# A three-layer CIN on one core: the weight tables built on the chip instead of gathered from HBM, and the first input tiles fetched by halves

## The chip, the core and the metric

The kernel runs on one core of one Trainium2 chip. The core has five engines that run side by side and wait for each other by semaphores: TensorE (PE, matrix products into PSUM), VectorE (DVE), ScalarE (ACT), GpSimd (POOL) and SyncE (SP), and 16 DMA engines that all queues share. The metric is device time of one launch in microseconds (us), lower is better. Everything is float32; each f32 matmul stands in the trace as two TensorE records.

## The reference, cut to what matters

```python
B, F, E, H = 1024, 39, 64, 64          # x is (1024, 39, 64); O = Hk = 64
def _cin_layer(Xk, X0, W, b):
    Wr = W.reshape(O, Hk, Fdim)
    return jnp.einsum('bhe,bfe,ohf->boe', Xk, X0, Wr) + b[None, :, None]
Xk = X0
for W, b in ((W0, b0), (W1, b1), (W2, b2)):
    Xk = _cin_layer(Xk, X0, W, b)
    outs.append(Xk.sum(axis=-1))
return jnp.concatenate(outs, axis=-1) @ fc_w.T + fc_b
```

Only linear sums of layers 2 and 3 are needed, so the kernel folds W1, W2 and fc_w into one table T. For each pair of fields (a, b) there is then one row of 128 weights, `T[a, b, 0:64]` beside `W0[a, b, 0:64]`. Because the product x_a·x_b is symmetric, the row for (a, b) is added to the row for (b, a). The hot loop multiplies pairs of rows of x (VectorE) and multiplies the products by these weights (TensorE).

## The kernel before

x is cut into 32 blocks of 2048 columns (32 samples of 64). A block is first copied to a DRAM table `xd` with one row for each field, and then GpSimd gathers four tiles of 128 rows, each a different list of fields (`rt`), so that six products of two tiles cover most pairs; a seventh product (`ut`·`vt`) covers the rest for two blocks at once. So two blocks have 13 steps: 12 of four full matmuls and one of eight half ones.

```python
def gather_rows(dst, n, k):
    table = xd[n // 2 % NTAB][: FT if k < 4 else 2 * FT]
    nc.gpsimd.indirect_dma_start(
        dst, None, table, bass.IndirectOffsetOnAxis(ap=lists[:, k : k + 1], axis=0))

def product(n, c):                       # VectorE, 128x2048
    p = prods.tile([128, BLK], F32, name="p", tag="p")
    ...nc.vector.tensor_tensor(p, rt[n % 2][:, i], rt[n % 2][:, k], ALU.mult)...

def multiply(n, c, p, quarters=range(BLK // MM)):     # TensorE, 512 columns each
    ...nc.tensor.matmul(po[n + h][m], wa[w, c, :], p[w, bass.ts(m, MM)], start=..., stop=...)
```

The weights go through DRAM. T is made by TensorE out of `w1s` and `v2`, joined with W0 in `part` and `rest`, stored as a DRAM table of 1600 rows, and gathered back twice for each of the seven chunks (the row of (a, b) into `wa`, that of (b, a) into `wb`); VectorE adds the two.

```python
for s, copy in enumerate((nc.vector.tensor_copy, nc.scalar.copy)):
    ...copy(part[:, :, at], pt[s]...); copy(rest[:, 0:NR, at], pr[s]...)
nc.sync.dma_start(tablev[:, 0:NA, :], part[0:FT])
nc.scalar.dma_start(tablev[:, NA : 2 * NA, :], part[H : H + FT])
nc.sync.dma_start(tablev[:, 2 * NA : FT, :], rest[0:FT])
...
def weights(c):
    for k, w in enumerate((wa, wb)):
        nc.gpsimd.indirect_dma_start(w[:, c], None, table[:],
            bass.IndirectOffsetOnAxis(ap=wlists[:, k, c : c + 1], axis=0))

weights(0); weights(1); weights(3)       # one GpSimd queue for weights and tiles
roll(1, (2,)); weights(2); roll(0, (3,)); weights(4); weights(5)
roll_half(0); weights(6); roll(1, (3,))
load(2); load(3)
...
nc.vector.tensor_tensor(wa[:, c], wa[:, c], wb[:, c], ALU.add)
```

The steps of the first two blocks are interleaved (three of block 0, three of block 1, then the rest), so that weights that come late are asked for late. `spin(n)` issues n matmuls of zeros into a bank that nobody reads. After that the loop is the same for all blocks: multiply step s, make the product of step s + 4, and at a block's end add its bias, multiply and reduce (`finish`, on ACT and DVE), then gather the tiles of block n + 2.

Of the kernel before, what the change touches and what calls it, by code (L numbers as in the profile page):

```python
# [57 lines left out]
FH = F * H  # L59
NG = 3  # L60
# [14 lines left out]
NA = 16  # L75
NR = F - 2 * NA
# [4 lines left out]
NONE = FT * FT - 1  # L81
# [14 lines left out]
def cin_kernel(ctx: ExitStack, tc: tile.TileContext, x, w0t, b0, w1, b1, w2, b2, fc_w, fc_b, out):  # L96
# [23 lines left out]
    def gather_rows(dst, n, k):  # L120
        table = xd[n // 2 % NTAB][: FT if k < 4 else 2 * FT]
        nc.gpsimd.indirect_dma_start(  # L122
            dst, None, table, bass.IndirectOffsetOnAxis(ap=lists[:, k : k + 1], axis=0)
        )

    def roll(n, tiles=range(4)):
        for i in tiles:
            gather_rows(rt[n % 2][:, i], n, n % 2 * 4 + i)
# [6 lines left out]
    wb = const.tile([128, NCHUNK, 2 * H], F32, name="wb")  # L135
    fc = const.tile([H, 3], F32, name="fc")
    v2 = const.tile([128, H], F32, name="v2")
    bias = const.tile([H, 2], F32, name="bias")
    b0s = const.tile([128, 1], F32, name="b0s")
# [5 lines left out]
    wlists = const.tile([128, 2, NCHUNK], I32, name="wlists")  # L145
# [4 lines left out]
    table = dram.tile([FT * FT, 2 * H], F32, name="table")  # L150
    tablev = table.rearrange("(b a) h -> b a h", a=FT)

    prep = tc.tile_pool(name="prep", bufs=1)
    with prep as prep:
        w2s = prep.tile([128, FH // 2], F32, name="w2s")
        w1s = prep.tile([128, FH // 2], F32, name="w1s")
        fc2 = prep.tile([128, 32], F32, name="fc2")
        ones = prep.tile([16, 128], F32, name="ones")
        zeros = prep.tile([128, MM], F32, name="zeros")
        w0s = prep.tile([128, NA * H], F32, name="w0s")  # L160
        w0r = prep.tile([H, NR * H], F32, name="w0r")
        part = prep.tile([128, NA, 2 * H], F32, name="part")
        rest = prep.tile([H, NR + 1, 2 * H], F32, name="rest")
        place = prep.tile([128, 1], I32, name="place")
        warm = prep.tile([1, 1], F32, name="warm")
# [3 lines left out]
        nc.vector.memset(warm, 0.0)  # L169
        nc.vector.memset(zeros, 0.0)  # L170
        nc.vector.memset(fc2, 0.0)  # L171
        nc.vector.memset(ones, 1.0)
        load(0, nc.gpsimd)
        nc.gpsimd.memset(w0s, 0.0)
        nc.gpsimd.memset(w0r, 0.0)
        load(1, nc.gpsimd)
        nc.gpsimd.memset(v2, 0.0)
        nc.gpsimd.memset(rest[:, NR], 0.0)

        def halves(dst, w):  # L180
            for s in range(2):
                nc.sync.dma_start(
                    dst[H * s : H * s + H], w[:, s * (FH // 2) : (s + 1) * (FH // 2)]
                )

        def load_ones(k, engine):
            for row in (F, FT + F):
                engine.dma_start(xd[k][row].rearrange("(p c) -> p c", c=128), ones)

        halves(w2s, w2)  # L190
        halves(w1s, w1)
        nc.scalar.dma_start(fc, fc_w.rearrange("o (l h) -> h (o l)", h=H))
        load_ones(0, nc.scalar)
        nc.scalar.copy(warm, warm)
        for k in range(2):
            nc.scalar.dma_start(w0s[H * k : H * k + F], w0t[:, NA * k : NA * (k + 1), :])
        nc.scalar.dma_start(w0r[0:F], w0t[:, 2 * NA : F, :])
        for s in range(2):
            nc.scalar.copy(fc2[H * s : H * s + H, 0:1], fc[:, 2:3])  # L199
            nc.scalar.copy(v2[H * s : H * s + H, F:FT], fc[:, 1:2])  # L200
        for k, t in enumerate((b1, b2)):
            nc.sync.dma_start(bias[:, k : k + 1], t.rearrange("(h o) -> h o", o=1))
        nc.sync.dma_start(b0s[H:128], b0.rearrange("(h o) -> h o", o=1))
        nc.sync.dma_start(fcb, fc_b.rearrange("(p o) -> p o", o=1))


        idle = bank("idle")

# [4 lines left out]
        spin(2)  # L213


        tmp = prep.tile([128, 16], F32, name="tmp")
        fields_of = prep.tile([128, 6], F32, name="fields_of")
        scaled = prep.tile([128, 6], F32, name="scaled")
# [16 lines left out]
        row, j, extra, t, half, q = new(), new(), new(), new(), new(), new()  # L235
        field = [fields_of[:, i : i + 1] for i in range(6)]
        nc.vector.tensor_copy(row, place)
        nc.vector.tensor_scalar(third, place, 171, None, ALU.mult)
        nc.vector.tensor_scalar(third, third, 9, None, ALU.logical_shift_right)
        nc.vector.tensor_copy(field[0], third)  # L240
        fused(j, field[0], -float(NG), row, ALU.mult, ALU.add)
        step(row, K, 1.0, extra)
        for i in (1, 2, 3):
            f = field[i]
            fused(f, j, float(STEP[i]), field[0], ALU.mult, ALU.add)
            step(f, F - BASE[i], -float(F), t)
            fused(f, f, float(BASE[i]), t, ALU.add, ALU.add)
            fused(t, row, float(EXTRA[i] - K), f, ALU.add, ALU.subtract)
            fused(f, t, extra, f, ALU.mult, ALU.add)
        nc.vector.tensor_scalar(t, field[0], -1.0, float(F), ALU.mult, ALU.add)  # L250
        fused(field[0], t, extra, field[0], ALU.mult, ALU.add)
        nc.vector.tensor_copy(lists[:, 0:4], fields_of[:, 0:4])
        nc.vector.tensor_scalar(lists[:, 4:8], fields_of[:, 0:4], float(FT), None, ALU.add)
        roll(0, (0, 1, 2))
        roll(1, (0, 1))
# [9 lines left out]

        nc.vector.tensor_scalar(half, half, float(FT), None, ALU.mult)
        nc.vector.tensor_scalar(lists[:, 8:10], fields_of[:, 4:6], half, None, ALU.add)

        blocks = prep.tile([H, F * 32], F32, name="blocks")
        w2v = w2s.rearrange("p (h f) -> p f h", f=F)
        pv = [bank("pv") for _ in range(2)]
        for k in range(2):
            for u in range(4):
                rows = slice(u % 2 * H, u % 2 * H + H)
                f0 = u // 2 * 19 + k * 10
                nc.tensor.matmul(  # L278
                    pv[k][32 * u : 32 * u + 32, 0:320],
                    fc2[rows],  # L280
                    w2v[rows, f0 : f0 + 10, :],
                    start=True,
                    stop=True,
                )
        spin(1)
        for k in range(2):
            for u in range(2):
                f0 = u * 19 + k * 10
                nc.vector.transpose(  # L289
                    blocks[:, 32 * f0 : 32 * (f0 + 10)], pv[k][H * u : H * u + H, 0:320]  # L290
                )
        column = blocks.rearrange("h (f j) -> h f j", j=32)[:, :, 0]
        nc.vector.tensor_copy(v2[0:H, 0:F], column)
        nc.scalar.copy(v2[H:128, 0:F], column)
        nc.scalar.copy(part[:, :, H : 2 * H], w0s.rearrange("b (a h) -> b a h", h=H))
        nc.scalar.copy(rest[:, 0:NR, H : 2 * H], w0r.rearrange("b (a h) -> b a h", h=H))


        nc.vector.tensor_scalar(scaled, fields_of, float(FT), None, ALU.mult)
        pair = prep.tile([128, 4], F32, name="pair")  # L300
        nc.vector.tensor_scalar(wlists[:, 0, 0:3], scaled[:, 1:4], field[0], None, ALU.add)
        nc.vector.tensor_scalar(wlists[:, 1, 0:3], fields_of[:, 1:4], scaled[:, 0:1], None, ALU.add)
        nc.vector.tensor_tensor(wlists[:, 0, 3:5], scaled[:, 2:4], fields_of[:, 1:3], ALU.add)
        nc.vector.tensor_tensor(wlists[:, 1, 3:5], scaled[:, 1:3], fields_of[:, 2:4], ALU.add)
        for m, (i, k) in enumerate(((1, 3), (3, 1), (4, 5), (5, 4))):
            nc.vector.tensor_tensor(pair[:, m : m + 1], scaled[:, k : k + 1], field[i], ALU.add)
        fused(wlists[:, 0, 5:6], extra, float(NONE), pair[:, 0:1], ALU.mult, ALU.max)
        fused(wlists[:, 1, 5:6], extra, float(NONE), pair[:, 1:2], ALU.mult, ALU.max)
        last = step(q, 62, float(NONE))
        nc.vector.tensor_tensor(wlists[:, 0, 6:7], pair[:, 2:3], last, ALU.max)  # L310
        nc.vector.tensor_scalar(t, q, float(F), float(NONE), ALU.is_lt, ALU.mult)
        nc.vector.tensor_tensor(pair[:, 3:4], pair[:, 3:4], t, ALU.max)
        nc.vector.tensor_tensor(wlists[:, 1, 6:7], pair[:, 3:4], last, ALU.max)


        w1v = w1s.rearrange("o (h f) -> o f h", f=F)
        pt = [bank("pt") for _ in range(2)]
        pr = [bank("pr") for _ in range(2)]
        for s in range(2):
            rows = slice(H * s, H * s + H)  # L320
            for k in range(2):
                nc.tensor.matmul(  # L322
                    pt[s][H * k : H * k + H],
                    v2[rows],
                    w1v[rows, NA * k : NA * (k + 1), :],
                    start=True,
                    stop=True,
                )
        for s in range(2):
            rows = slice(H * s, H * s + H)  # L330
            nc.tensor.matmul(  # L331
                pr[s][rows, 0 : 32 * NR], v2[rows], w1v[rows, 2 * NA : F, :], start=True, stop=True
            )
# [15 lines left out]
    def weights(c):  # L349
        for k, w in enumerate((wa, wb)):  # L350
            nc.gpsimd.indirect_dma_start(  # L351
                w[:, c], None, table[:], bass.IndirectOffsetOnAxis(ap=wlists[:, k, c : c + 1], axis=0)
            )

    weights(0)
    weights(1)
    weights(3)
    roll(1, (2,))
    weights(2)
    roll(0, (3,))  # L360
    weights(4)
    weights(5)
    roll_half(0)
# [191 lines left out]
```

## Time and profile before

| what | value |
|---|---|
| device time, median of 3 runs (range) | 768.59 us (768.55 to 769.1) |
| span of the profiled run, mean TensorE clock granted | 766.5 us, 0.991 |
| busy: PE, DVE, ACT, POOL | 745.1, 641.2, 160.4, 320.4 us |
| first matmul of the hot loop starts | 33.13 us |
| its last ones end | about 761.5 us |

Span and waits come from one profiled execution, the time from runs without a profile. The span is 2.1 us shorter than the device time. A group of instructions in the profile gives busy time, mean ns of one, idle time of its engine before them and what ended it. "PEld" is TensorE's weight load, which overlaps its matmuls. PEclk is the clock that the throttle granted, 1.00 is full speed.

### The profile page before, as it was taken

To read this page: it belongs to the slowest core of one execution; us is meant where nothing else is said; L and a number is where in the kernel's file an instruction comes from. 1 tells how busy PE (TensorE), PEld (TensorE's weight loads), DVE (VectorE), ACT (ScalarE), POOL (GpSimd) and SP (SyncE) were. 2 spreads that over 40 slices of the span, in tenths; PEclk is the share of its full clock that TensorE was granted. 3 is DMA by queue.
4 is the path that set the end of the run, shared out by engine and by line. 5 is a ranking of instruction groups with operands and counts; after the bars stand their busy time and mean duration, and the time that the engine had idled before them with its cause. 6 is when DMAs were issued, how large, how long until landed. Compare 5 with 4: busy or idle time off the path is not lost.

```text
span 766.5 us, 5146 instructions
## 1 busy us (share of the span) xinstructions
PE 745.1 (97%) x1856; PEld 322.3 (42%) x1856; DVE 641.2 (84%) x479; ACT 160.4 (21%) x207; POOL 320.4 (42%) x185
## 2 busy tenths in 40 slices
PE   6597999999999999999999999999999999999998
PEld 2243444444444444444444444444444444444443
DVE  5375988889888889888889988888988888998885
ACT  2002312122221212222121222112122221112212
POOL 4487273542436244253634325363442636334200
PEclk9899999999999999999999999999999999999999
DMA  8849958576865757676575777657577764737400
GB/s 260 268 151 384 402 183 342 168 273 231 327 240 203 283 170 276 244 316 241 189 287 183 276 254 292 256 178 284 185 297 252 267 260 147 284 150 317 165 0 0
DMA packets 62839, 181.79 MB, mean 237 GB/s; under 512 B 41364, under 2 KB 41499, under 8 KB 42254
## 3 DMA queue, kind: packets, MB, share of 16 engines
q0 software_dynamic: 23712, 169.34, 57.5%
q1 hardware_dynamic: 38494, 11.36, 6.4%
q10 hardware_dynamic: 608, 0.77, 0.3%
q8 instruction: 14, 0.23, 0.1%
q14 instruction: 11, 0.09, 0.0%
HBM read 180.58 MB, written 11.10 MB: 250 GB/s over the span
## 4 chain that ended last, share of the span: by engine, by line
PE 91%; DMA 3%; issue 2%; POOL 2%; DVE 1%; ACT 0%; DVEq 0%; POOLq 0%; SPq 0%
PE po L391 91%; DMA table<-rest 1%; POOL wa L351 1%; DMA u<-xd,lists 1%; POOL wb L351 1%; DMA wb<-table,wlists 0%; PE pt L322 0%; DVE blocks L289 0%; POOL r L122 0%; DVE fields_of L233 0%; DVE tmp L229 0%; DVE tmp L233 0%; PE pr L331 0%; DVE g L430 0%; DVE sums L432 0%
## 5 line engine op out<-in xcount | busy, mean ns | idle before, releaser
L391 PE MATMUL po<-p,wa 128*128 128x512 f32 (+1 forms) x1792 | 724.3, 597 | 11.9 <-DVE wa L471 11.9
L377 DVE TENSOR_TENSOR p<-r 128x2048 f32<-128x2048 f32 x192 | 434.5, 2291 | 88.1 <-PE po L391 82.2
L391 PEld LDWEIGHTS po<-p,wa 128*128 128x128 f32 (+1 forms) x1792 | 315.0, 190 | 420.4 <-issue 395.4
L122 POOL DMA_INDIRECT r<-xd,lists x128 | 249.3, 1948 | 366.0 <-DVE p L377 340.0
L410 ACT ACTIVATE x<-po,b0s 64x512 f32<-64x512 f32 x124 | 84.5, 684 | 356.4 <-PE po L391 349.8
L404 ACT COPY g<-u 39x1024 f32<-39x1024 f32 x64 | 66.6, 1043 | 216.2 <-DVE sums L421 181.2
L416 DVE SCALAR_TENSOR_TENSOR g<-po,fc,x 64x512 f32<-64x512 f32 x124 | 86.4, 734 | 0.0
L421 DVE TENSOR_REDUCE sums<-g 103x16 f32<-103x1024 f32 x62 | 75.6, 1220 | 2.2
L379 DVE TENSOR_TENSOR p<-u,v 128x2048 f32<-128x2048 f32 x16 | 36.5, 2284 | 9.1 <-DMA v<-xd,lists 9.1
L122 POOL DMA_INDIRECT u<-xd,lists x16 | 29.8, 1859 | 4.9 <-issue 4.6
L122 POOL DMA_INDIRECT v<-xd,lists x16 | 16.6, 1035 | 4.9 <-issue 4.9
L351 POOL DMA_INDIRECT wa<-table,wlists x7 | 11.0, 1573 | 14.6 <-DMA table<-rest 12.8
L211 PE MATMUL idle<-zeros 128*128 128x512 f32 x24 | 12.9, 686 | 1.5 <-DVE fc L171 1.5
L471 DVE TENSOR_TENSOR wa<-wa,wb 128x128 f32<-128x128 f32 x7 | 2.0, 291 | 11.6 <-DMA wb<-table,wlists 11.6
L351 POOL DMA_INDIRECT wb<-table,wlists x7 | 9.7, 1382 | 2.1 <-issue 2.1
L211 PEld LDWEIGHTS idle<-zeros 128*128 128x128 f32 x24 | 4.8, 212 | 8.2 <-issue 6.8
L430 DVE SCALAR_TENSOR_TENSOR g<-po,fc,x1q 64x512 f32<-64x512 f32 x4 | 3.0, 742 | 5.3 <-ACT x1q L429 5.3
L278 PE MATMUL pv<-w2s,fc 64*32 64x320 f32 x16 | 2.8, 764 | 4.5 <-ACT fc L199 4.5
L289 DVE STREAM_TRANSPOSE blocks<-pv 64x320 f32<-64x320 f32 x4 | 2.1, 514 | 3.7 <-issue 3.6
L429 ACT ACTIVATE x1q<-po,b0s 64x512 f32<-64x512 f32 x4 | 2.7, 684 | 10.2 <-PE po L391 10.2
L278 PEld LDWEIGHTS pv<-w2s,fc 64*32 64x32 f32 x16 | 1.0, 142 | 6.7 <-ACT fc L199 6.1
L432 DVE TENSOR_REDUCE sums<-g 103x8 f32<-103x512 f32 x4 | 2.7, 686 | 0.1
(74 smaller groups left out, 30.0 us busy)
## 6 DMA issues: line engine op xcount, KB each, us to landing
xd<-in_x SPq DMA_DIRECT2D x30, 312.0 KB
r<-xd,lists POOLq DMA_INDIRECT x128
w2s<-in_w SPq DMA_DIRECT2D x2, 312.0 KB
xd<-in_x POOLq DMA_DIRECT2D x2, 312.0 KB
w1s<-in_w SPq DMA_DIRECT2D x2, 312.0 KB
table<-part SPq DMA_DIRECT2D x1, 320.0 KB
table<-part ACTq DMA_DIRECT2D x1, 320.0 KB
w0s<-in_w0t ACTq DMA_DIRECT2D x2, 156.0 KB
```

Source lines behind the costliest of these rows:

```text
L122: nc.gpsimd.indirect_dma_start(dst, None, table, bass.IndirectOffsetOnAxis(ap=lists[:, k : k + 1], axis=0))
L211: nc.tensor.matmul(idle, zeros[:, 0:128], zeros, start=True, stop=True)
L278: nc.tensor.matmul(pv[k][32 * u : 32 * u + 32, 0:320], fc2[rows], w2v[rows, f0 : f0 + 10, :], start=True, stop=True,)
L351: nc.gpsimd.indirect_dma_start(w[:, c], None, table[:], bass.IndirectOffsetOnAxis(ap=wlists[:, k, c : c + 1], axis=0))
L377: nc.vector.tensor_tensor(p, rt[n % 2][:, i], rt[n % 2][:, k], ALU.mult)
L379: nc.vector.tensor_tensor(p, ut[n // 2 % 2], vt[n // 2 % 2], ALU.mult)
L391: nc.tensor.matmul(po[n + h][m], wa[w, c, :], p[w, bass.ts(m, MM)], start=c == opens[n + h], stop=c == closes[n + h],)
L404: nc.scalar.copy(gt[H : H + F], ut[n // 2 % 2][h : h + F, bass.ts(m, SUB)])
L410: nc.scalar.activation(x1[m // 2][:, bass.ts(m % 2, MM)], po[n][m][H:128], AF.Identity, bias=b0s[H:128])
L416: nc.vector.scalar_tensor_tensor(gt[0:H, at], po[n][m][0:H], fc[:, 0:1], x1[m // 2][:, at], ALU.add, ALU.mult)
L421: nc.vector.tensor_reduce(sums[:, b_at : b_at + SB], gt.rearrange("p (b e) -> p b e", e=E), AX.X, ALU.add)
L430: nc.vector.scalar_tensor_tensor(gt[0:H], po[n][m][0:H], fc[:, 0:1], t, ALU.add, ALU.mult)
```

## The change

It is for the opening. The DRAM table of weights, its 14 gathers, `wb`, and the lists of rows go away. Instead `both` holds the same table in SBUF, with h on the partitions (W0's 64 and T's 64) and the pair (a, b) along the row. A chunk's rows lie on diagonals of that table, so VectorE adds pieces of a diagonal to their mirror images into `pairs`, TensorE turns the 128x128 chunk, and ACT copies it to `wa`. W0's half of `both` comes from 39 TensorE transposes, T's half from 39 small matmuls. The first three tiles of block 0 are gathered by halves of 1024 columns and the first products are made by halves; block 0's steps now all come before block 1's. The first load moves from GpSimd's queue to ACT's, GpSimd's second load goes behind the first gathers, fc_w is loaded as one row and turned by TensorE, and 12 spins become three. W0 and T trade places in the 128 columns; `finish` is otherwise as it was.

```diff
+        for cols in halves:
+            roll(0, (0, 1, 2), cols)
+        load(1, nc.gpsimd)
+        roll(0, (3,))
 ...
+        roll(1, (0, 1))
+        roll_half(0)
+        roll(1, (2, 3))
+        load(2, nc.gpsimd)
+        load(3, nc.gpsimd)
 ...
-        nc.sync.dma_start(tablev[:, 0:NA, :], part[0:FT])
-        nc.scalar.dma_start(tablev[:, NA : 2 * NA, :], part[H : H + FT])
-        nc.sync.dma_start(tablev[:, 2 * NA : FT, :], rest[0:FT])
 ...
+        for a in range(F):
+            nc.tensor.transpose(at_field(a, 0)[:, 0:F], w0s[:, a * H : a * H + H], unit[0:F, 0:F])
+        for a in range(F):
+            nc.tensor.matmul(at_field(a, H), w1v[:, a, :], v2, start=True, stop=True)
+        for g in range(4):
+            at = slice(g * NG0 * FT, min((g + 1) * NG0, F) * FT)
+            copy = (nc.vector.tensor_copy, nc.scalar.copy)[g % 2]
+            copy(both[:, at], pt[g][:, 0 : at.stop - at.start])
+        spin(1)
 ...
-    weights(0)
-    weights(1)
-    weights(3)
-    roll(1, (2,))
 ...(and the rest of that list)
+    def weight_rows(c):
+        def put(at, by, n, a, b, sa, sb, twice=True):
 ...
+                nc.vector.tensor_tensor(
+                    out, diagonal(a, b, sa, sb), diagonal(b, a, sb, sa), ALU.add
+                )
 ...
+        for j in range(NG):
+            a, b = STEP[i] * j + BASE[i], STEP[k] * j + BASE[k]
+            cuts = sorted({0, F - a, F - b, F})
+            for lo, hi in zip(cuts, cuts[1:]):
+                put(NG * lo + j, NG, hi - lo, (a + lo) % F, (b + lo) % F, 1, 1)
+    def weight_turn(c):
 ...
+        nc.tensor.transpose(tr[:, at], pairs[:, c], unit)
+        nc.scalar.copy(wa[:, c], tr[:, at])
 ...
+    weight_rows(0)
+    weight_turn(0)
+    for k, (n, c) in enumerate(steps[:3]):
+        if k:
+            weight_rows(c)
+        p[n, c] = prods.tile([128, BLK], F32, name="p", tag="p")
+        product(n, c, halves[0], p[n, c])
+    for n, c in steps[:3]:
+        product(n, c, halves[1], p[n, c])
+    n, c = steps[3]
+    weight_rows(c)
+    p[n, c] = product(n, c)
+    for k, (n, c) in enumerate(steps[:3]):
+        multiply(n, c, p[n, c], (0,))
+        if k < 2:
+            weight_turn(steps[k + 1][1])
+        multiply(n, c, p[n, c], (1,))
```

In the loop the rows of chunks 5 to 7 are made just ahead of the product that needs them, and each turn stands after the first matmul of the step before.

## The prediction

> **What bounds the kernel now.** I read the page's first part, the costliest groups, ACT's timeline for the loop's period, then the chain of waits and the timeline of the first 70 us. First the page: engine totals, and the loop's matmuls and products.
>
> ```profile
> PE 745.1 (97%) x1856; PEld 322.3 (42%) x1856; DVE 641.2 (84%) x479; ACT 160.4 (21%) x207; POOL 320.4 (42%) x185
> ...
> L391 PE MATMUL po<-p,wa 128*128 128x512 f32 (+1 forms) x1792 | 724.3, 597 | 11.9 <-DVE wa L471 11.9
> L377 DVE TENSOR_TENSOR p<-r 128x2048 f32<-128x2048 f32 x192 | 434.5, 2291 | 88.1 <-PE po L391 82.2
> ```
>
> TensorE is the bound: ahead of the loop's matmuls it idled 11.9 us in all, for weights. VectorE waits for TensorE (82.2 us), not the reverse. ACT's timeline shows the period of two blocks, since ACT takes a block's banks as soon as TensorE closes them:
>
> ```profile
> 197.78 1.49 ACT L410 ACTIVATE x<-po,b0s 64x512 f32<-64x512 f32 x2 [13.16 <-PE po L391]
> ...
> 242.82 1.48 ACT L410 ACTIVATE x<-po,b0s 64x512 f32<-64x512 f32 x2 [13.16 <-PE po L391]
> ```
>
> That is 45.04 us for two blocks, 3.46 us a step, and it repeats unchanged to the end. Sixteen pairs are 16 x 45.03 = 720.5 us that the change doesn't touch. What is left is the opening. The chain of waits, in order of time:
>
> ```profile
> 17.07 0.35 ACT rest L338
> 17.49 10.15 DMA table<-rest
> 27.67 0.70 issue
> 28.36 0.95 POOL wa L351
> ...
> 29.62 0.42 POOL wb L351
> ...
> 53.30 7.05 DMA u<-xd,lists
> ...
> 66.10 0.30 DVE wa L471
> 66.44 695.02 PE po L391 x1728
> ```
>
> The weights are ready in SBUF at 17.4; 10.15 us go into storing the table, and five more into gathering it. Later the same queue of GpSimd, with weights and tiles in turn, brings u and then the last chunk so late (53.3 to 66.1) that TensorE waits once more. The timeline has the first product of the loop's matmuls, and the second stall:
>
> ```profile
> 19.17 2.29 DVE L377 TENSOR_TENSOR p<-r 128x2048 f32<-128x2048 f32 x1 [1.83 <-DMA r<-xd,lists]
> ...
> 33.13 12.08 PE L391 MATMUL po<-p,wa 128*128 128x512 f32 x24 [7.85 <-DVE wa L471]
> ...
> 66.44 34.12 PE L391 MATMUL po<-p,wa 128*128 128x512 f32 x82 [4.06 <-DVE wa L471]
> ```
>
> The first product starts at 19.17, so the inputs are there 14 us ahead of the weights. The stretch by stretch view shows the clock:
>
> ```profile
> 33.00:34.00 1.00, 0.87 (x1) 0.50 (x2) 1.00 (x1) 0.00 (x0) 0.70 (x2) 0.50 0.98 181
> ...
> 37.00:38.00 1.00, 1.00 (x4) 0.47 (x3) 0.00 (x0) 0.00 (x0) 0.69 (x2) 1.00 0.10 29
> ```
>
> At half clock (0.50, the third last column) for about 3.4 us after each of the two stalls, a loss of some 1.7 us each. So the balance is: start 33.1, plus 720.5, plus 4.06 idle and two half-clock stretches (together 7.8), ends at 761.4; the tail to 766.5 and 2.1 outside the span are 7.2 more: 768.6.
>
> **What the Trainium skill says.** (1) "TensorE: Matmul & The Clock Gate", Part 1: the clock starts at half rate, is released by some 3.4 us of activity, and falls back after idling. The trace agrees: 0.50 at 33 us, 1.00 from 37. Its Part 4 adds that transposes on TensorE may not count as activity; no instruction of the kernel before shows it. (2) The same page, "LDWEIGHTS": a load costs by its columns, P/1.2 ns, so 53 ns for 64. The trace has 131 ns for a 64-column f32 load, 190 ns for 128 and 78 ns for one, all at full clock: some 77 ns fixed and 0.9 ns a column. (3) "TensorEngine Tiling (Array Packing)", "Instruction Overhead": about 60 cycles a matmul however narrow. This bears on the 78 narrow products that are new. (4) "DMA: Bandwidth & Descriptors", "Anatomy of one DMA": about 2.0 us fixed beside the bytes. The table's way out and back pays this twice, and its 10.15 us for 800 KB are longer than that formula, since the queues were full (DMA share about 1.0 from 5 to 25 us).
>
> **Part by part.**
>
> *Removed.* The store (10.15 us), its issue gaps and the gathers up to the first addition: from 17.4 to 33.1, 15.7 us of the chain. Further on, twelve weight gathers that delay tiles on GpSimd's queue (about 1.25 to 2.2 us each), and with them the stall of 4.06 us at 62 to 66 and its cold stretch of 1.9.
>
> *When can weights exist now?* The loads ahead of the gathers are w2, w1 and one block of x, 1.6 MB against 1.93 MB before, with w0's 0.4 MB behind them. The profile moves 119 GB/s in the first 5 us and 267 in the next. I take w2 as landed at 7 (fc_w as one row no longer holds it up; before, the pv products waited until 9.77 on ACT). The pv products took 2.84 us at half clock; the same columns again: 10. Two VectorE transposes and copies, where four took 2.2 us: v2 at 11.2. Meanwhile TensorE turns W0: 39 transposes, then 39 matmuls x 2 records = 78. A pass has a 64-column load and 40 columns of moving data. Loads overlap the matmul before (in the loop a 190 ns load disappears in 433 ns records). Between full overlap (0.9 x 64 = 58 ns) and the whole 131 ns of a load I choose 90 ns: 39 x 90 = 3.5 us and 78 x 90 = 7.0 us. Whether a transpose is one record or two isn't shown in this trace; I take one. 10 + 3.5 + 7.0 = 20.5. A last short copy 0.3, six diagonal additions of about 0.1 us (four independent 128x1 additions take 0.42 us in this trace), 0.7 with a gap, then a first half product of 1.17 us (half of 2.29); the turn and its copy, some 0.6, lie beside that product. First matmul at about **22.5 us**, against 33.1.
>
> *Inputs.* Six half gathers of 0.5 MB, 1.25 us of GpSimd each, start when block 0 has landed, 7 to 9 us. At the 330 to 420 GB/s of this stretch all 3 MB are in by 18 to 19. So the halves are ahead of the weights and don't set the start.
>
> *Added after the start.* VectorE makes rows (0.6 to 1.0 us a chunk) among half products: rows and second half 2.0 us after the first, third 2.2 after that, while two matmuls take 1.7: about 0.7 us of TensorE gaps. Then the products come at 3.3 us a step, TensorE needs 3.46. Six turns on TensorE at 0.3 us (190 ns load and 128 columns): 1.8. One spin at full clock stands in the gap, so I count half of a cold stretch: 0.9. Tiles: tile 3, four more gathers and the rest are 8 MB from 19 us at 400 GB/s, u and v in by 34, needed near 38: no stall. Together 3.5 to 4.
>
> *Sum.* 22.5 + 720.5 + 4 + 7.2 = 754.2. I allow 0.8 for what a longer list of dependent starts usually adds: **755.0 us**, that is 13.6 less (1.8%).
>
> **Rivals.** (A) *The narrow passes are the new chain.* If a transpose is two records and a pass costs 131 ns or runs at half clock (few spins are left, and light passes may not release the clock), 117 to 156 passes take 15 to 20 us instead of 10.5, and the first matmul comes at 28 to 32: 760 to 765. For it: cold 128-column loads measure 340 ns here, and the pv products ran wholly at 0.50. Against: the store-and-gather detour it replaces was 15.7 us. (B) *Everything fits, and the inputs set the start.* Gathering by halves is only worth its trouble if tiles are late against weights; if passes take 60 ns, weights are done at 17, the first matmul comes at 18.5 to 19.5 and the time is 750 to 751. For it: the 39-column loads at 24.9 us follow each other within 80 ns. (C) *VectorE becomes the bound of the first block.* Some 50 strided additions on a path that also makes products; at 0.17 us each instead of 0.1 they add 3.5 us, of which a step's slack eats little: 757 to 758. (D) *The gain is returned later* because a tile comes late in blocks 1 to 3 or a PSUM bank is still held by the turned chunks: one stall of 3 to 5 us and a cold stretch, 759 to 761. The loop has no slack to recover anything, as TensorE sets every period.
>
> **Range and chances.** B pulls to 750, A to 763, C and D by a few us up. I give 748.5 to 762.0 for 8 in 10. The 2% line is near 753.4, a little below my centre, and B lies under it: 0.41 for faster by over 2%, 0.57 within 2%, 0.02 slower by over 2%; the last would need a start later than 45 us.
>
> **What would show it.** The period between ACT's block ends must stay 45.03 us; if not, the whole balance is wrong. The loop's first matmul should start at 19 to 26 us, waiting for VectorE's first half product, and no stall over 1.5 us should stand later. The 117 narrow passes should cost 60 to 130 ns each from start to start; over 10.5 us in all means A. The gathered halves must have landed before the first product is ready to go; if the product waits for DMA, B's view of inputs holds. Diagonal additions near 0.1 us refute C. I am wrong altogether if the new chain of preparation is longer than 30 us.

## The result, and the profile after

The changed kernel takes 756.75 us (median of 4 runs, 756.49 to 757.34) against 768.83 for the kernel before: a ratio of 0.984, 95% interval 0.983 to 0.986. That is 12.1 us less; 755.0 had been predicted, with a range of 748.5 to 762.0. The span of the profiled run is 754.8 us, the mean granted clock 0.990.

The page of the changed kernel, first its engine totals, then groups of instructions (busy us, mean ns of one, idle time ahead and what ended it):

```profile
PE 747.9 (99%) x1968; PEld 331.6 (44%) x1968; DVE 641.7 (85%) x506; ACT 160.9 (21%) x216; POOL 318.1 (42%) x184
...
L418 PE MATMUL po<-p,wa 128*128 128x512 f32 (+1 forms) x1792 | 723.2, 596 | 0.4 <-ACT wa L392 0.4
...
L339 PE MATMUL pt<-v,w1s 64*64 64x40 f32 x78 | 9.6, 312 | 0.0
...
L339 PEld LDWEIGHTS pt<-v,w1s 64*64 64x64 f32 x78 | 9.5, 213 | 0.1
...
L356 DVE TENSOR_TENSOR pairs<-both 128x6 f32<-128x6 f32 (+27 forms) x50 | 5.4, 175 | 0.4 <-ACT both L343 0.4
```

L418 is the loop's matmul (L391 before). Its idle time went from 11.9 us to 0.4: once the loop has begun, TensorE waits for no weights. The busy time is the same within 1.1 us. TensorE now has 112 more records, nearly all ahead of the loop. ACT's timeline shows that the loop itself is untouched:

```profile
71.56 1.48 ACT L437 ACTIVATE z<-po,fc0s 64x512 f32<-64x512 f32 x2 [9.29 <-PE po L418]
...
116.59 1.48 ACT L437 ACTIVATE z<-po,fc0s 64x512 f32<-64x512 f32 x2 [9.70 <-PE po L418]
```

Two blocks take 45.03 us, as before. The chain of waits (start, us, what), from the first spin on:

```profile
6.97 2.00 PE idle L210 x2
8.98 2.51 PE pv L305 x14
11.48 0.94 PE pt L333 x8
12.43 1.50 PE pt L337 x39
13.93 9.54 PE pt L339 x78
23.47 2.00 PE idle L210 x2
25.47 0.23 PE tr L391
...
25.72 0.27 ACT wa L392
...
26.04 2.07 PE po L418 x2
...
49.61 699.92 PE po L418 x1744
```

Compare this with the chain shown of before. No DMA stands in it from there to the end; the table's 10.15 us, its gathers and the 7.05 us of `u` are gone. In their place stands TensorE itself, from 7 to 26: the products for v2 (L305), zero products that clear the banks (L333), 39 transposes (L337), 78 narrow passes (L339), and twice a spin (L210). The loop begins at 26.04 instead of 33.13 (7.1 us), and from there to the end of its matmuls (749.5) it takes 723.5 us instead of 728.3 (4.8 us). These two make 11.9 of the 12.1 us. Of 723.5, 720.5 are the sixteen periods, so 3.0 us are lost after the start. The stretch by stretch view (after the span: busy share and count of PE, PEld, DVE, ACT, POOL, then the clock, DMA share, GB/s) has the larger part of that:

```profile
14.00:15.00 1.00, 1.00 (x10) 1.00 (x10) 0.00 (x0) 0.00 (x0) 0.92 (x1) 1.00 0.89 267
15.00:16.00 1.00, 1.00 (x11) 1.00 (x10) 0.00 (x0) 0.00 (x0) 0.77 (x1) 0.93 0.56 119
16.00:17.00 1.00, 1.00 (x10) 1.00 (x10) 0.00 (x0) 0.00 (x0) 0.69 (x2) 0.50 0.76 301
...
29.00:30.00 1.00, 1.00 (x3) 0.50 (x2) 1.00 (x2) 0.00 (x0) 1.00 (x1) 0.74 0.54 172
```

The clock falls to half near 15.9 us, in the middle of the narrow passes and with TensorE busy all the time, and comes back at about 29.5: 3.5 us of the loop at half speed lose some 1.8. Six turns at 0.11 to 0.21 us and three tiny products before 49.6 are another 1.1.

### The profile page after: what moved, and what is told of

Same layout as the page of the kernel before. It is cut to its first block, busy times and chain, and to the rows that moved or that the text cites. A ratio compares the mean times of both kernels' runs of the same rounds, so it can differ in the third digit from the quotient of the medians.

```text
span 754.8 us, 5372 instructions
## 1 busy us (share of the span) xinstructions
PE 747.9 (99%) x1968; PEld 331.6 (44%) x1968; DVE 641.7 (85%) x506; ACT 160.9 (21%) x216; POOL 318.1 (42%) x184
## 4 chain that ended last, share of the span: by engine, by line
PE 99%; DVE 1%; ACT 0%; issue 0%
PE po L418 96%; PE pt L339 1%; PE idle L210 1%; PE pv L305 0%; PE pt L337 0%; PE tr L391 0%; PE pt L333 0%; DVE g L457 0%; PE small L271 0%; DVE sums L459 0%; ACT zq L456 0%; PE small L267 0%; DVE zeros L184 0%; PE small L277 0%; DVE fcrow L265 0%
## 5 line engine op out<-in xcount | busy, mean ns | idle before, releaser
L418 PE MATMUL po<-p,wa 128*128 128x512 f32 (+1 forms) x1792 | 723.2, 596 | 0.4 <-ACT wa L392 0.4
L404 DVE TENSOR_TENSOR p<-r 128x2048 f32<-128x2048 f32 (+1 forms) x195 | 434.7, 2257 | 84.5 <-PE po L418 84.5
L418 PEld LDWEIGHTS po<-p,wa 128*128 128x128 f32 (+1 forms) x1792 | 314.5, 190 | 405.7 <-issue 384.2
L123 POOL DMA_INDIRECT r<-xd,lists x131 | 255.8, 1952 | 373.5 <-DVE p L404 326.6
L437 ACT ACTIVATE z<-po,fc0s 64x512 f32<-64x512 f32 x124 | 84.3, 683 | 356.5 <-PE po L418 349.7
L443 DVE SCALAR_TENSOR_TENSOR g<-po,b0s,z 64x512 f32<-64x512 f32 x124 | 86.3, 734 | 0.0
L123 POOL DMA_INDIRECT v<-xd,lists x16 | 25.8, 1612 | 4.9 <-issue 4.6
L339 PE MATMUL pt<-v,w1s 64*64 64x40 f32 x78 | 9.6, 312 | 0.0
L339 PEld LDWEIGHTS pt<-v,w1s 64*64 64x64 f32 x78 | 9.5, 213 | 0.1
L210 PE MATMUL idle<-zeros 128*128 128x512 f32 x6 | 6.2, 1140 | 1.7 <-DVE zeros L184 1.7
L356 DVE TENSOR_TENSOR pairs<-both 128x6 f32<-128x6 f32 (+27 forms) x50 | 5.4, 175 | 0.4 <-ACT both L343 0.4
L116 POOL DMA_DIRECT2D xd<-in_x x5 | 5.2, 1056 | 0.0
L456 ACT ACTIVATE zq<-po,fc0s 64x512 f32<-64x512 f32 x4 | 2.7, 683 | 10.2 <-PE po L418 10.2
```

What stands on the lines that cost most here:

```text
L116: engine.dma_start(xd[n // 2 % NTAB][first : first + F].rearrange("f (b e) -> f b e", e=E), xv[:, n * BB : (n + 1) * BB, :],)
L123: nc.gpsimd.indirect_dma_start(dst[:, cols], None, table, bass.IndirectOffsetOnAxis(ap=lists[:, k : k + 1], axis=0), element_offset=cols.s ...
L210: nc.tensor.matmul(idle, zeros[:, 0:128], zeros, start=True, stop=True)
L339: nc.tensor.matmul(at_field(a, H), w1v[:, a, :], v2, start=True, stop=True)
L356: nc.vector.tensor_tensor(out, diagonal(a, b, sa, sb), diagonal(b, a, sb, sa), ALU.add)
L404: nc.vector.tensor_tensor(p[:, cols], r[:, i, cols], r[:, k, cols], ALU.mult)
```

## The experiments

Three theories were open. **Chain:** the start is the sum of TensorE's small work, so each microsecond taken out of it comes off the time; within it either the stride of the weights in `w1s` (39 floats) or the half clock makes the passes dear. **Inputs:** the tiles set the start, so the chain is hidden. **Contention:** something beside the chain, the gathers above all, disturbs it. Kernels 1 to 4 ran on one chip, 5 to 8 on a second, 9 to 12 on a third, each beside the kernel before (767.93, 767.58, 768.31 us).

| kernel | time, us (range) | ratio to before (95%) | profiled run: first loop matmul | its device time less that start |
|---|---|---|---|---|
| changed kernel | 756.75 (756.49 to 757.34) | 0.984 (0.983 to 0.986) | 26.04 | 730.6 |
| 1 no spins | 758.74 (758.09 to 759.87) | 0.988 (0.986 to 0.990) | 28.16 | 731.7 |
| 2 contiguous weights | 758.15 (758.13 to 758.56) | 0.988 (0.986 to 0.990) | 28.26 | 729.9 |
| 3 without T | 754.69 (754.13 to 755.15) | 0.983 (0.981 to 0.985) | 22.66 | 731.5 |
| 4 whole gathers | 756.22 (755.41 to 756.92) | 0.985 (0.983 to 0.987) | 26.04 | 729.4 |
| 5 whole gathers and products | 758.78 (758.73 to 759.43) | 0.989 (0.987 to 0.992) | 27.69 | 731.7 |
| 6 gathers after the table | 761.84 (759.97 to 765.89) | 0.992 (0.989 to 0.995) | 30.99 | 734.9 |
| 7 five wide products | 761.26 (758.95 to 763.66) | 0.993 (0.989 to 0.996) | 29.66 | 730.8 |
| 8 the same, no spins | 759.08 (758.52 to 759.84) | 0.990 (0.987 to 0.992) | 28.21 | 731.6 |
| 9 first products early | 760.27 (759.06 to 761.35) | 0.990 (0.988 to 0.992) | 28.65 | 731.1 |
| 10 T ahead of W0 | 757.64 (756.49 to 758.37) | 0.987 (0.985 to 0.989) | 26.18 | 730.3 |
| 11 whole gathers, no spins | 757.08 (756.81 to 757.24) | 0.986 (0.984 to 0.987) | 25.30 | 731.7 |
| 12 changed kernel again | 759.17 (758.84 to 760.51) | 0.989 (0.987 to 0.990) | 30.07 | 730.4 |

The last column holds the whole study together: whatever is done to the opening, what comes after the start costs 729.4 to 731.7 us (number 6 has a late stall). The start decides the time, so the question is what decides the start. Within the 2.3 us of this column, it is mostly the length of the half-clock stretch that differs: 1.0 us after the start in kernel 4, 5.8 in kernel 11.

A caution for what follows: the changed kernel was measured on two occasions, and the times don't overlap (756.49 to 757.34, and 758.84 to 760.51 as number 12), though the kernel before took 768.83 and 768.31 beside them. Differences of about 2 us count only between kernels of one chip, and the changed kernel itself ran beside 9 to 11 alone.

**1. The spins ahead of the v2 products and after the table left out.**

```diff
-        spin(1)          # before the v2 products
...
-        spin(1)          # after the copies of the table
```

> The two spins after the first are left out. Chain theory (one queue of TensorE work ahead of the loop sets the start, and the time follows it one to one): the pv products start at 7.0 to 7.6 us instead of 8.98 if w2 has landed by then, and the last spin no longer stands between the diagonal additions and the first turn: first matmul of the loop at 23.8 to 24.4 instead of 26.04, time 754.5. If w2 lands only near 9, the last spin alone is gained: 756.4. Rival, clock: the spins are what lifts the clock; without them the loop's first stretch at half clock gets up to 2 us longer and eats the gain: 756 to 758.

Measured: 758.74 us. The v2 products start at 6.91, two microseconds earlier, so w2 was there and the spin had stood in front of it. But then the transposes wait 1.62 us for W0, which lands at 11.9, and start at 11.96 instead of 12.36: 0.4 of the 2 us is left. After that the narrow passes take 12.3 us instead of 9.5, since TensorE stops among them three times without a wait that the profile shows (0.40, 0.85 and 0.50 us, "issue"), with groups of only 3 to 5 passes between. The time lies above the range of the rival too. On this trace leaving the spins out gains nothing; what it is worth without the stops, kernel 11 shows.

**2. Weights of the narrow passes contiguous.** W1 is handed over laid out as (o, f, h); nothing else changes.

```diff
-        w1v = w1s.rearrange("o (h f) -> o f h", f=F)
+        w1v = w1s.rearrange("o (f h) -> o f h", h=H)
```

> w1 is laid out in memory with h innermost, so the weights of the 39 narrow products are 64 neighbouring floats instead of every 39th; nothing else changes. Stride theory: the 212 ns of these weight loads, the same before and after the clock fell at 15.9 us, come from the stride; contiguous they take 131 ns as in the kernel before, the 78 passes 5 us instead of 9.5, time 752 to 752.5. Rival, clock: at half clock contiguous 64-column loads take 222 to 227 ns as well (the zero and fc products), so only the passes before 15.9 get faster: the 78 passes take 8 to 9.5 us, time 755.5 to 756.7.

Measured: 758.15 us. Here is what the stride costs. The statistics of the weight loads (min/median/max ns of a record) in the changed kernel between 14.6 and 15.3 us, at full clock by the view above:

```profile
L339 PEld LDWEIGHTS pt<-v,w1s x8: 212/213/220, 14.4 to 15.3; 64*64 64x64 f32 x8
```

and the same of kernel 2, also at full clock:

```profile
L339 PEld LDWEIGHTS pt<-v,w1s x14: 135/135/135, 14.5 to 15.2; 64*64 64x64 f32 x14
```

A load of 64 columns takes 135 ns when its elements lie side by side and 212 when they are 39 floats apart, and the passes follow each other in 67 ns (21 in 1.41 us) instead of 122. At half clock the loads no longer differ that way: 223 ns contiguous in kernels 2 and 6, 212 with the stride in the changed kernel; the passes still do, 107 ns apart in kernel 6 against 122. The time fits neither range: in kernel 2 the gain is lost at once. Gaps of 0.20 to 0.78 us follow from 15.7 to 21, the clock falls, and the last 37 passes need 4.65 us.

**3. T left out.** The 39 narrow products are not made (the outputs lack T's part); W0's transposes take 128 columns so that the table is full.

```diff
-        for a in range(F):
-            nc.tensor.matmul(at_field(a, H), w1v[:, a, :], v2, start=True, stop=True)
```

> Leaves out the 39 narrow products (W0's transposes take 128 columns instead of 64, so T's place holds the next field's W0, and the output is not the reference's). Chain theory: 9.5 us leave the chain, first matmul at 17 to 17.5, and if nothing else binds the time is 747.5 to 748. Rival, inputs: the halves gathered first are in at about 17.5 and the second halves at about 23, so the loop starts at 18.5 to 19 or waits for the second halves, 750 to 751. Clock rival: the time stays above 754 because the loop starts cold and stays cold longer.

Measured: 754.69 us, 2.1 less than the changed kernel's first measurement, and 1.5 to 4.1 less than 1, 2 and 4 beside it, though 9.5 us of TensorE's chain are gone. The timeline says where they went (in brackets: idle before, and what ended it):

```profile
12.63 2.60 PE L337 MATMUL pt<-unit,w0s 39*128 39x39 f32 x39
13.76 0.66 DVE L345 COPY both<-pt 128x480 f32<-128x480 f32 x1 [1.48 <-PE pt L337]
...
18.89 0.66 DVE L345 COPY both<-pt 128x480 f32<-128x480 f32 x1 [4.47 <-remote]
20.32 0.26 ACT L345 COPY both<-pt 128x120 f32<-128x120 f32 x1 [3.77 <-remote]
...
21.52 0.44 PE L393 MATMUL tr<-unit,pairs 128*128 128x128 f32 x1 [4.42 <-issue]
```

TensorE is done with the table at 15.2, but VectorE copies its third part at 18.89 and ACT its last at 20.32. "Remote" is the profile's word for a release that no instruction of the trace explains. So a late release of 4 us stands where the work was. This speaks against a pure chain, and for something beside it between 15 and 21 us. The inputs theory falls too: the first product starts at 21.29 right behind the rows, not behind a transfer. And the number, which lies where the clock rival put it, doesn't make that rival right: after the start this kernel needs 731.5 us, only 0.9 more than the changed one.

**4. The first tiles gathered whole**, the products still by halves.

```diff
-        for cols in halves:
-            roll(0, (0, 1, 2), cols)
+        roll(0, (0, 1, 2))
```

> The first three tiles are gathered whole again, the products still come by halves. Chain theory: tiles 0 and 1 are in by 21 us, before the first product at 24.5, so nothing changes: 756.4 to 757.2. Rival, inputs: the start slips by what the gathers by halves had gained, 1 to 3 us: 758 to 760.

Measured: 756.22 us. The 78 passes run in one piece (9.79 us), the start is 26.04, the same as in the changed kernel. So gathering by halves brings nothing here: no first product waits for a tile. Beside 1 and 2, which gather by halves on the same chip and have gaps among the passes, it is even 2.5 and 1.9 us faster.

**5. Whole gathers and whole first products.** As 4, and each first product is made in one instruction.

```diff
-        p[n, c] = prods.tile([128, BLK], F32, name="p", tag="p")
-        product(n, c, halves[0], p[n, c])
-    for n, c in steps[:3]:
-        product(n, c, halves[1], p[n, c])
+        p[n, c] = product(n, c)
```

> Whole gathers and whole first products, the new weights kept. Chain theory: the first product takes 2.29 us instead of 1.22 after the rows are there, so the start slips by 1.0 us: 757.2 to 757.9 (756.2 with whole gathers alone). Rival (halves are what the change gains by): 760 or more.

Measured: 758.78 us. The first product takes 2.28 instead of 1.22 us, and the start is 27.69: 1.65 later than in 4. Of that 0.8 us are already there when the first row is added (24.64 instead of 23.85), mostly two gaps of TensorE (0.20 us before the last transpose, 0.53 after the fourth pass). The other 0.9 is the product: the first matmul now waits for it, where in 4 it waited for the turned weights. Making the products by halves is worth its place.

**6. Contiguous weights, and no gather beside the passes.** As 2, but the lists of fields, and with them all gathers, come after the table's copies.

```diff
+        nc.vector.tensor_copy(lists[:, 0:4], fields_of[:, 0:4])   # moved behind the copies
+        for cols in halves:
+            roll(0, (0, 1, 2), cols)
 ...(and the other gathers and loads of that list)
```

> The contiguous w1 again, but the lists that the gathers read are written only after the table has been copied out, so that no gather runs beside the narrow products (the inputs then come late, and the time itself must be longer, 762 to 766). Contention theory: the 4 to 5 us of gaps among the narrow products from 15.7 to 21 us, and the first copy of the table released 6 us late, come from the gathers that fill the DMA engines then; without them the 78 passes take 5 to 7 us in one piece and the copies follow at once. Rival (clock, or the supply of instructions by their number): the gaps stand at the same passes as before.

Measured: 761.84 us; the late inputs cost more than they save, as they must here. What counts is the stretch in question:

```profile
13.55 8.33 PE L328 MATMUL pt<-v,w1s 64*64 64x40 f32 x78
16.16 0.66 DVE L332 COPY both<-pt 128x480 f32<-128x480 f32 x1 [4.15 <-PE pt L328]
...
21.28 0.66 DVE L332 COPY both<-pt 128x480 f32<-128x480 f32 x1 [4.46 <-PE pt L328]
...
29.62 1.22 DVE L404 TENSOR_TENSOR p<-r 128x1024 f32<-128x1024 f32 x1 [6.58 <-DMA r<-xd,lists]
```

One piece without a gap, every copy as soon as its group is written. Against kernel 2, which differs in the gathers alone but ran on another chip, this fits contention: the gaps and late releases are gone with the gathers. It also bounds the stride: the passes take 8.33 us, not the 5 to 7 expected, against 9.54 with the stride, since 74 of the 78 run at half clock.

**7 and 8. Five wide products instead of 39 narrow ones.** v2 becomes the weights, 512 columns of W1 pass in each product, and 39 transposes of 128 columns then turn W0 and T together; 8 leaves the spins out too.

```diff
+                nc.tensor.matmul(pw[k][H * u : H * u + H, 0 : n * H], v2, w1v[:, a : a + n, :],
+                    start=True, stop=True)
...
+            nc.tensor.transpose(pt[a // NG0][:, ...FT], part[lo : lo + FT, a % 24], unit[...])
```

> T is made by five wide products (448 to 512 columns, v2 as the weights), copied beside W0 into one tile with b on the partitions, and 39 transposes of 128 columns turn both halves at once; spins as in the changed kernel. Narrow-product theory: wide products 2.6 us at half clock, copies 1.1, transposes 2.6 (67 ns each, as in the run without T), instead of 0.9 + 1.5 + 9.5: first matmul at 21.3 instead of 26.0, time 752. If the stall that comes with the gathers hits this chain as well (3 to 4 us in the run without T), first matmul at 24.5 and 755.

> The same without the second and third spins. Chain theory: pv products at 6.9 instead of 8.9, so everything 2 us earlier where W0 has landed (11.9 holds the transposes, not the wide products): first matmul at 19.5 to 20.5, time 750 to 751. Stall theory: the chain then meets the first gathers sooner or stalls as long, the start stays at 23 to 25 and the time at 753.5 to 755.5. Clock rival: a longer stretch at half clock, up to 2 us lost after the start.

Measured: 761.26 and 759.08 us, both misses. Part is an accident of my edit: the loads of W0 into `part` hold ACT's queue, ACT's copies of fc come at 11.25 and 11.63 instead of 6.34, and the v2 products start at 13.80 and 12.18. But from v2 to the full table it also takes 10.2 and 10.4 us against 11.4: the wide products cost 5.84 and 5.89 us (I had counted half), and the copies between and 3.98 us of transposes come on top. So the wide form as a whole gains one microsecond on this path.

**9. First products between the table's copies.** The first three half products are made on VectorE between its two table copies, and the last spin goes.

```diff
+            if g == 2:
+                for c in ORDER[:3]:
+                    i, k = PAIRS[c]
+                    early[c] = prods.tile([128, BLK], F32, name="p", tag="p")
+                    nc.vector.tensor_tensor(early[c][:, 0:SUB], rt[0][:, i, 0:SUB], rt[0][:, k, 0:SUB], ALU.mult)
```

> The first halves of the first three products are moved on VectorE to stand between its two copies of the table (it sat idle there from 17.7 to 22.8 us), and the last spin is left out. If the inputs are there ahead of the weights, as the prediction held, the three products end by 23 without holding the second copy, the first matmul no longer waits for a product or the spin and starts at 25.2 to 25.5 instead of 26.04, and the gaps of TensorE between the first halves go: time 755.2 to 755.9. Rival (the halves come only just in time): the second copy waits behind a product that waits for its tile, and the time is 757 or more.

Measured: 760.27 us. The passes show four gaps (0.16 to 0.74 us) between 16 and 19.6, VectorE's first table copy is released at 21.31, 9.05 us after the work ahead of it ("remote"), and the three products run from 21.89 to 25.4, in time: the second copy still waits 0.54 us for TensorE's passes. So moving the products costs nothing, but the gaps hold the table, and with it the start (28.65), so there is nothing to gain either.

**10. T's products ahead of W0's transposes**, group by group, on top of 9 and without the spin ahead of the v2 products.

```diff
+            for a in mine:
+                nc.tensor.matmul(at_field(a, H), w1v[:, a, :], v2, start=True, stop=True)
+            for a in mine:
+                nc.tensor.transpose(at_field(a, 0)[:, 0:F], w0s[:, a * H : a * H + H], unit[0:F, 0:F])
```

> The same, and also without the spin ahead of the pv products, and group by group with the narrow products ahead of W0's transposes, so that they start as soon as v2 is there (10.4) and not when w0 has landed (11.9). Chain theory: table complete at 21.5 to 22, first matmul at 23.4 to 24, time 753.7 to 754.5. Contention theory: the narrow products that still run after 14 us are held up by the gathers as in the run without the two spins, and the time is 756 to 758.

Measured: 757.64 us. The passes start at 10.39 instead of 13.9, since W0 is asked for later. Yet the start is 26.18: the clock falls to half at 12.1, and 12 transposes take 0.91 to 0.98 us, twice as long as at full clock (24 strided passes take 3.10 us before and after the fall); VectorE's early products wait for tiles (3.21 and 1.11 us), and one ACT copy comes 11.32 us after ACT's work before it, again "remote". The time lies in the range of contention, but the passes have only one gap, of 0.22 us, so it is not the mechanism that this range stood for.

**11 and 12. Whole gathers without the spins, and the changed kernel itself, on the same chip.** 11 is 4 with the two edits of 1.

> Whole gathers together with no second and third spin. If the gaps among the narrow products come from gathers by halves (4 KB rows), they don't appear and the 2 us of the spin are gained: 754 to 754.7. If they come from any gather beside narrow products that start earlier, gaps of 3 to 5 us as in the run with halves: 757 to 759.

> The changed kernel once more, beside the others on the same chip, to have differences of 1 us or less from the same place: 756.5 to 757.4, first matmul at 26.0.

Measured: 757.08 and 759.17 us; the ranges lie 1.6 us apart. The timeline of 12, the changed kernel to the letter:

```profile
14.10 1.40 PE L339 MATMUL pt<-v,w1s 64*64 64x40 f32 x10
15.95 0.59 PE L339 MATMUL pt<-v,w1s 64*64 64x40 f32 x4 [0.45 <-issue]
17.40 0.69 PE L339 MATMUL pt<-v,w1s 64*64 64x40 f32 x4 [0.87 <-issue]
18.84 0.48 PE L339 MATMUL pt<-v,w1s 64*64 64x40 f32 x3 [0.74 <-issue]
...
20.27 7.23 PE L339 MATMUL pt<-v,w1s 64*64 64x40 f32 x56 [0.49 <-issue]
21.98 0.66 DVE L343 COPY both<-pt 128x480 f32<-128x480 f32 x1 [9.71 <-PE pt L339]
```

and of 11:

```profile
13.34 9.58 PE L337 MATMUL pt<-v,w1s 64*64 64x40 f32 x78
```

In 12 only 22 passes run between 14.1 and 20.3, and the start is 30.07; in 11 all 78 take 9.58 us and the start is 25.30. So the profile of the changed kernel shown first is one without the disturbance, and its 756.75 us are the better side of this kernel. Since all timed runs of one occasion lie apart from all of the other, what decides between the two goes with the chip or the occasion, not with the single execution; the record can't say which.

The time of 11 lies in the range meant for gaps, yet it has none: of the spin's 2 us, 1.43 go to waiting for W0 (landed at 11.86). What 4 and 11 share is the whole gathers. Each has the lowest median of the complete kernels on its chip and no gap among the passes, one with the spins and one without; the kernels by halves beside them (1, 2, 9, 12, slightly 10) have gaps, again with spins and without. So the first tiles gathered whole and the products made by halves are the version these runs point to. Taking the spins out doesn't add to it: 4 has the ratio 0.985 and 11 has 0.986; 11 starts 0.7 us earlier and then loses more at half clock (731.7 after the start against 729.4).

## Why the prediction was right in kind and 1.75 us off

**What held.** The period stays at 45.03 us; the tail and what lies outside the span are 7.2 us; w2 has landed by 6.9 (predicted 7); the transpose is one record; the inputs are ahead (rival B: no product waits for a tile, and taking 9.5 us out of the chain uncovers no transfer). They are ahead by less than was predicted, though: GpSimd starts the half gathers at 11.34 us, not at 7 to 9, and they land from 15.5 to 25.0, not by 18 to 19. The first product's tiles are there at 20.1 and it starts at 24.48, so a chain shortened by more than some 4 us would meet the inputs; in kernel 10 the early products do wait for them. The six additions of the first diagonal rows take 0.71 us, ten take 1.01: 0.1 us each, so rival C falls. The page's mean of 175 ns counts the overlap of pipelined instructions. No weight or tile comes late in the first blocks (rival D): VectorE waits 2.4 us for `v` once, and TensorE doesn't stop for it.

**What was mis-sized.** Term by term, against the sum of the prediction (whose balance of the kernel before has a slip: 4.06 and twice 1.7 make 7.5, not 7.8, so 0.3 us stayed unexplained):

| term | predicted | measured | difference |
|---|---|---|---|
| v2 products done | 10 | 11.5 | +1.5 |
| zero products that clear the banks | none | 0.94 | +0.9 |
| 39 transposes | 3.5 | 1.5 | -2.0 |
| 78 narrow passes | 7.0 | 9.54 | +2.5 |
| table done to first matmul | 2.0 | 2.6 | +0.6 |
| losses after the start | 4.8 (4 + 0.8 allowed) | 3.0 | -1.8 |

The sum is +1.7. That it is so small is partly luck: errors of 5.5 us up and 3.8 down stand behind it, and the same kernel's 759.17 us on the other occasion would have been 4.2 off. The largest term that failed is "I choose 90 ns" for a pass. It was taken between figures of contiguous loads at full clock. Here the load is strided (212 ns even at full clock, against 131 in the trace before), and the passes are 122 ns apart. By the prediction's own sign (transposes and passes over 10.5 us mean A) the 11.0 us measured are rival A, of a smaller size: one record for a transpose, and a start at 26.04 instead of 28 to 32. But its half clock, which did come two microseconds into the passes, is not what made them long: the loads take 212 ns and the passes stand 122 ns apart after the fall of the clock as before it. It is the stride, and without it the half clock would take most of its place (107 ns in kernel 6).

The Trainium skill's "TensorE: Matmul & The Clock Gate", Part 4, which the prediction cited, says that transposes may not count as activity. This trace shows more than that: the clock fell during ordinary matmuls, narrow ones, at 100% busy, and stayed at 0.50 through the 7.6 us of them that followed. For transposes the trace gives 38 ns from start to start at full clock, so the 90 ns (the loads' figure again) were too dear by more than half.

The first line of the table is the spin: it is behind the small products in TensorE's queue, and the v2 products, whose data are there at 6.9, stand behind it until 8.98. I had seen the spins and counted only their good. After the start the half clock lost 1.8 us where I had counted 0.9, but the turns took 0.8 instead of 1.8, and the gaps (0.7) and the allowance (0.8) didn't come: ahead of the loop's matmuls TensorE idled 0.4 us, all of it before the first.

**What the prediction didn't have at all** is the disturbance between 15 and 21 us. It appears with gathers by halves in kernels 1, 2, 9 and 12 as gaps, slightly in 10, in 3 as late releases, but not among the wide products of 7 and 8; with whole gathers there is none in 4 and 11, and two gaps in 5; without gathers, none in 6. The changed kernel shows both. Taken between 12 and the first profile of the same kernel it is worth 4.0 us of start.

That it belongs to the gathers is what 6 against 2 speaks for, and that gathering by halves favours it, what 4 against 1 and 2, and 11 against 9 and 12, speak for; there is one profile of each. But the gathers alone don't make it, and full DMA engines don't either. From 15.4 to 20.3 us the two profiles of the changed kernel agree in the DMA engines' share (0.87) and in GpSimd's busy time (3.98 us), and yet TensorE is busy for 4.90 us in one and 2.11 in the other; in kernel 11 the share is 0.99, with no gap. The queue called "instruction" moves one packet between 13 and 21 us in both, too. What delays a matmul's issue or a semaphore's release stays open.

## What to carry to other kernels

A table that goes out to DRAM only to be picked up in another order is worth building in place, even by a hundred tiny TensorE instructions: here 15.7 us of round trip became some 12 us of TensorE work, and the transfers left the chain with it. Size such chains at the clock and the stride they will really have, and look for what stands ahead in the queue; but don't expect that each microsecond taken out of them comes off the end (without 9.5 us of products the start came 3.4 us earlier, and without 2 us of spin 0.7, in kernel 11 against 4). When one kernel differs by 2 us between two occasions, measure it beside its variants on the same one before explaining any of them.

## What the runs showed of the hardware that was not expected

- A 64-column f32 weight load takes 135 ns with its elements side by side and 212 ns at a stride of 39 floats, at full clock; at half clock 223 and 212.
- Narrow passes follow each other in 67 ns (contiguous, full clock), 107 (contiguous, mostly half clock) or 122 to 129 (strided, either clock). f32 transposes of 64 columns: 38 ns at full clock, 77 at half; of 128 columns 67 (2.60 us for 39).
- TensorE busy without a pause is not enough to hold or lift the clock: it fell at 15.9 us in the changed kernel, at 13.8 in kernel 6 and 14.1 in kernel 11, each time during the narrow passes, and at 12.1 in kernel 10, during passes that no transpose of W0 had come before. In the changed kernel it then stayed at 0.50 to the end of the passes, 7.6 us later.
- The clock's column can't be read before its first change: it prints 1.00 at 7 us in the changed kernel, but the spin there takes 1.0 us a record, the same as the one at 23.47 with a granted 0.50. That the clock had come up before it fell at 15.9 is seen in the transposes from 12.4 on, 38 ns apart against 77 in kernel 10 at 0.50.
- While gathers are issued, TensorE paused 0.2 to 0.9 us between matmuls that wait for nothing in the profile (kernels 1, 2, 9, 12), and in kernel 3 a copy was released 4 us after its data were written. The groups of passes between the pauses often start at an even spacing (15.95, 17.40, 18.84 and 20.27 us in kernel 12; 16.94, 18.36 and 19.80 in kernel 1).
